# Row maxima of latent attention taken over pairs of key blocks, with ScalarE's positive part between TensorE and VectorE

## The chip, the cores and the metric

The kernel runs on one core of a Trainium2 chip. The metric is the device time of one execution in microseconds (us). A program is timed in several runs, and the median is given. One more execution is recorded by the profiler; its span runs from the first to the last instruction of the core.

The core has TensorE (PE, matrix products into PSUM; "PEld" are its weight loads), VectorE (DVE), ScalarE (ACT), GpSimd (POOL), and SyncE (SP), which issues transfers. Each works through its own queue in order and waits for others by semaphores.

## The reference

Eight blocks of a small hybrid network run on x of shape (2, 1024, 128), each with a layer norm in front and the residual added behind. The first one is a causal latent attention, and the change lies in it alone:

```
q      = einsum('bld,dhk->blhk', x, Wq)              # 16 heads of 64
latent = einsum('bld,dc->blc', x, Wkv_down)          # 32 values per token
k, v   = latent through Wk_up, Wv_up                 # per head
attn   = softmax(where(key <= query, q.k / 8, min))  # over the keys
out    = (attn . v) through Wout
```

It is followed by a spiking feed-forward block, a state-space block, the spiking block again, a linear attention, an expert feed-forward, an attention with 16 heads of 8, and the experts again. All is in float32.

## The kernel before

The keys' up-projection is folded into the queries, so that a head's score is a product over the 32 latent values. Four heads (`J = 4`) lie on the 128 partitions, 32 each, and there are four such groups (`C = 4`). `qT[b]` holds the folded queries of batch b as (4 heads x 32) x group x 1024 tokens. `latT[b]` holds the latent values, repeated for the four heads, as 128 x 1024.

Softmax needs the maximum of each row of scores first. `row_maxima(b, seq, ps, together)` computes them for one batch and is the function that is changed. It goes over the eight query blocks `i` of 128 tokens (`TPB = 8`), the four groups `c`, and the keys up to the diagonal, `nk = (i + 1) * 128`, in halves of at most 512. One round of the innermost loop is called a step here; there are 48 for a batch, and each ends in a `yield`. In a step:

- TensorE makes the scores of four heads (line 265), 128 queries x up to 512 keys each, every head in its own bank of PSUM. The four heads use different rows of the array. In the trace, each of these float32 products is two instructions.
- If the half holds the diagonal block, TensorE adds the causal mask there (line 274): a product of an identity and a matrix that is -3.0e38 above the diagonal, both bf16.
- VectorE takes the negated maximum over the keys out of PSUM (line 283), for `together` heads in one instruction, and writes it into `nm`.

At the end of the batch, the two halves are merged (line 288), the maxima are split into three bf16 terms (lines 294 and 297) and transposed by TensorE into `nmT` (lines 301 and 302). `attend` then computes the scores again, transposed, adds `nmT` to them on TensorE (lines 355 and 364) and takes the exponentials on ScalarE (line 378).

The function is used twice.

- **Batch 0**: `together = 4`, two PSUM tiles of four banks. Nothing else is to be done then, and a scheduler orders the instructions.
- **Batch 1**: `together = 2`, three PSUM tiles of two banks, two of which a step needs. The order is written out by hand (`tc.manual_schedule`): `weave(into_space(0, bank), maxima, 1.1)` takes 1.1 steps of the maxima after each step of the first state-space work. That work has layer norms on VectorE and POOL, the spiking block's products with their activations (`f_ph` line 549, lines 551 and 552 on ScalarE, `f_py` line 557, thresholds on VectorE in line 569), and the state-space projections (`s_pm` line 618, evacuated by ScalarE in lines 678, 689 and 693 and by VectorE in lines 680, 687 and 698; step sizes in lines 705 to 715). Each engine gets its instructions in the order in which the two streams are drawn. What stands behind a waiting instruction in a queue waits too.

Everything behind the two stretches follows after them: `attend` of batch 0 after batch 0's maxima, and the state-space loop with `attend` of batch 1 after batch 1's.

Of the kernel before, what the change touches and what calls it, by code (L numbers as in the profile page):

```python
# [9 lines left out]
F32 = mybir.dt.float32  # L10
BF16 = mybir.dt.bfloat16
AF = mybir.ActivationFunctionType
ALU = mybir.AluOpType
AX = mybir.AxisListType
ENG = mybir.EngineType
PSUM = bass.MemoryType.PSUM
# [3 lines left out]
P = 128  # L20
# [4 lines left out]
TPB = L // P  # L25
# [103 lines left out]
def drain(steps):  # L129
    for _ in steps:  # L130
        pass
# [20 lines left out]
class LatentAttention:  # L152
# [3 lines left out]
    C, J, LD = 4, 4, 32  # L156
# [92 lines left out]
    def row_maxima(self, b, seq, ps, together):  # L249


        nc, C, J = self.g.nc, self.C, self.J
        qT, latT = self.qT[b], self.latT[b]

        nm = seq.tile([P, 2, TPB, C * J], F32, name="a0_nm")
        for i in range(TPB):
            nk = (i + 1) * P
            for c in range(C):
                for half, n0 in enumerate(range(0, nk, 512)):
                    n = min(nk - n0, 512)  # L260
                    last = n0 + n == nk
                    ss = [ps.tile([P, together, 512], F32, name="a0_s", tag="a0_s") for _ in range(J // together)]
                    for j in range(J):
                        quad = slice(32 * j, 32 * j + 32)
                        nc.tensor.matmul(  # L265
                            ss[j // together][:, j % together, :n],
                            qT[quad, c, bass.ts(i, P)],
                            latT[quad, n0 : n0 + n],
                            start=True,
                            stop=not last,  # L270
                        )
                    if last:
                        for j in range(J):
                            nc.tensor.matmul(  # L274
                                ss[j // together][:, j % together, n - P : n],
                                self.identb,
                                self.mask,
                                start=False,
                                stop=True,
                            )  # L280
                    for k, s in enumerate(ss):
                        h = c * J + k * together
                        nc.vector.tensor_reduce(  # L283
                            nm[:, half, i, h : h + together], s[:, :, :n], AX.X, ALU.max, negate=True
                        )
                    yield
        two = TPB // 2
        nc.vector.tensor_tensor(nm[:, 0, two:, :], nm[:, 0, two:, :], nm[:, 1, two:, :], ALU.min)
        terms = seq.tile([P, TPB, P], BF16, name="a0_terms")
        nc.gpsimd.memset(terms, 0.0)  # L290
        rest = nm[:, 0].rearrange("p i (c j) -> p i j c", c=C)
        for t in range(3):
            part = terms.rearrange("p i (j r) -> p i j r", j=J)[:, :, :, t : 3 * C : 3]
            nc.vector.tensor_copy(part, rest)
            if t < 2:
                left = seq.tile([P, TPB, J, C], F32, name=f"a0_left{t}")
                nc.vector.tensor_sub(left, rest, part)
                rest = left
        pt = ps.tile([P, TPB, P], BF16, name="a0_mt", tag="a0_s")
        for i in range(TPB):  # L300
            nc.tensor.transpose(pt[:, i, :], terms[:, i, :], self.identb)
        nc.vector.tensor_copy(self.nmT[b], pt.rearrange("p a b -> p (a b)"))
        yield
# [1183 lines left out]
def first_layer(g, w, open_experts, load_expert):  # L1487

    tc = g.tc

    def pool(stack, name, bufs, **kw):
        return stack.enter_context(tc.tile_pool(name=name, bufs=bufs, **kw))
# [7 lines left out]
    latent = LatentAttention(g, w, pool(latents, "a0_keep", 1, **right))  # L1500
    own = pool(latents, "a0_batch1", 1, **right)
    with ExitStack() as es:
        latent.project([pool(es, "a0_batch0", 1), own])
        with tc.tile_pool(name="a0_seq", bufs=1) as seq, tc.tile_pool(name="a0_ps_a", bufs=2, space=PSUM) as ps:
            drain(latent.row_maxima(0, seq, ps, 4))
        work = pool(es, "a0_work", 2)
        ps, ps_o = pool(es, "a0_ps_b", 3, space=PSUM), pool(es, "a0_ps_o", 1, space=PSUM)
        with tc.manual_schedule(engines=ALL):
            drain(latent.attend(0, work, ps, ps_o, added=True))
# [3 lines left out]
    seq = pool(spaces, "s_seq", 2)  # L1513
    dram = pool(spaces, "s_dram", 2, space=bass.MemoryType.DRAM)
    space = [StateSpace(g, w, b, shared, seq, dram) for b in range(B)]
# [40 lines left out]
    with tc.manual_schedule(engines=ALL):  # L1556
# [8 lines left out]
        ps, ps_o = pool(latents, "a0_ps_b", 2, space=PSUM, **right), pool(latents, "a0_ps_o", 1, space=PSUM, **right)  # L1565
# [23 lines left out]
def kernel(ctx: ExitStack, tc: tile.TileContext, d: dict, out: bass.AP):  # L1589
# [34 lines left out]
    def load_expert(e):  # L1624
        for name in ("Wg", "Wu"):
            nc.sync.dma_start(out=w[name][:, e, :], in_=d[name][e])
        nc.sync.dma_start(out=w["Wd"][:, e], in_=d["Wd"][e].rearrange("(c p) o -> p c o", p=P))

    first_layer(g, w, open_experts, load_expert)
    layer0.close()  # L1630
    heads_and_experts(g, w, [4, 5, 6, 7], [0, 1, 2, 3, 4, 5])
# [69 lines left out]
```

## Time and profile before

| | |
|---|---|
| median of 3 runs | 2143.78 us (2140.81 to 2145.67) |
| profiled execution: time, span | 2140.26 us, 2138.3 us |
| granted TensorE clock, mean | 0.941 of full speed |
| busy in the span: PE, DVE, ACT, POOL | 1849.9, 1590.4, 1145.6, 920.0 us |
| batch 0's maxima: first reduce to last reduce's end | 50.8 to 138.8 us |
| batch 1's maxima, woven into state-space work | 283.8 to 439.4 us |
| reduces of line 283, both batches | 144, 168.2 us busy on DVE |
| score products of line 265 | 768 matmul instructions, 118.1 us busy on PE |

Busy time is the time in which an engine has an instruction under way; register, branch and semaphore instructions do not count. The chain of waits follows the work that ended last back through the time and names at each place the engine that was waited for. A row of a group gives line, engine, operation, output and input with their shapes, the count, the busy time, the mean length of one in ns, and the engine's idle time before them with what ended it. In a stretch's row, the columns are busy time of PE, PEld, DVE, ACT and POOL, the granted clock, the share of the DMA engines and GB/s. Names in the profile leave out numbers: `a_s` are the score tiles, `a_nm` the maxima.

### The profile page before, as it was taken

The page shows a single profiled execution, that of the slowest core. Times are in us where ns is not written, and L with a number is a line of the kernel's source. Part 1 is how long each engine was busy: PE and PEld are TensorE (multiplying, and loading weights), DVE is VectorE, ACT ScalarE, POOL GpSimd, SP SyncE. Part 2 cuts the span into 40 slices and gives each one's busy share as a digit, 9 for nine tenths or more (in the row PEclk, how much of TensorE's full clock was granted, in tenths as well). Part 3 has the DMA queues.
Part 4 walks back from the last instruction along what each step waited for, and adds up shares of the span by engine and source line. Part 5 has one row for each costly group of instructions (what it writes and reads, how often), then busy time and mean ns, then how long its engine had stood idle before and what let it go on. Part 6 is the DMA issues. An engine that isn't in the chain of part 4 may idle for free.

```text
span 2138.3 us, 33736 instructions
## 1 busy us (share of the span) xinstructions
PE 1849.9 (87%) x13632; PEld 1063.0 (50%) x13632; DVE 1590.4 (74%) x1842; ACT 1145.6 (54%) x1577; POOL 920.0 (43%) x510
## 2 busy tenths in 40 slices
PE   7679978979977757899678899999899999998899
PEld 4223243323334422334356566676666666666753
DVE  5876866799765679896432798999899899998222
ACT  1016612266632457773433677777777777777422
POOL 1013411045321210000110288989889889998300
PEclk9979978989987978999899999999999999999999
DMA  4000000087653077660000466666666666666000
GB/s 93 1 1 2 1 1 1 10 208 180 157 117 118 11 166 178 157 151 7 0 1 0 110 177 160 176 178 175 162 173 175 173 175 177 173 178 172 11 5 6
DMA packets 73788, 220.00 MB, mean 103 GB/s; under 512 B 9184, under 2 KB 19872, under 8 KB 73504
## 3 DMA queue, kind: packets, MB, share of 16 engines
q1 hardware_dynamic: 54736, 149.40, 24.0%
q0 software_dynamic: 18432, 67.12, 16.5%
q8 instruction: 107, 1.75, 0.4%
q10 hardware_dynamic: 464, 1.33, 0.3%
q14 instruction: 49, 0.40, 0.1%
HBM read 78.35 MB, written 5.24 MB: 39 GB/s over the span
## 4 chain that ended last, share of the span: by engine, by line
PE 47%; DVE 28%; issue 8%; POOL 7%; ACT 5%; DMA 4%; SPq 0%; DVEq 0%; POOLq 0%; ACTq 0%
DVE h_e L1281 5%; DVE h_m L1275 5%; DVE a_nm L283 4%; POOL h_e L1331 4%; PE h_s L1264 4%; DVE s_h L792 3%; PE a_st L355 3%; PE a_s L265 3%; DMA h_e<-h_e 3%; PE e_pgu L1053 3%; PE e_pg L955 3%; PE e_pu L956 3%; PE e_po L971 3%; PE h_po L1111 3%; PE s_pm L618 3%
## 5 line engine op out<-in xcount | busy, mean ns | idle before, releaser
L1331 POOL TENSOR_TENSOR h_e<-h_e,h_r 128x2048 f32<-128x2048 f32 x128 | 601.5, 4705 | 76.3 <-ACT h_r L1324 42.4
L1284 ACT ACTIVATE h_e<-h_e 128x1024 f32<-128x1024 f32 x256 | 256.6, 1049 | 165.7 <-DVE h_e L1281 165.0
L1275 DVE TENSOR_REDUCE h_m<-h_s 128x128 f32<-128x2048 f32 x128 | 293.2, 2291 | 53.5 <-PE h_s L1264 50.7
L1281 DVE TENSOR_TENSOR h_e<-h_s,h_m 128x2048 f32<-128x2048 f32 x128 | 293.2, 2290 | 8.7
L381 POOL TENSOR_SCALAR_AFFINE_SELECT a_pT<-a_pT 128x256 f32<-128x256 f32 x120 | 126.0, 1071 | 209.2 <-ACT a_pT L378 206.3
L283 DVE TENSOR_REDUCE a_nm<-a_s 128x2 f32<-128x1024 f32 (+7 forms) x144 | 168.2, 1217 | 43.0 <-PE a_s L274 26.5
L1264 PE MATMUL h_s<-h_qz,h_kT 32*128 32x512 f32 x1024 | 148.0, 646 | 43.5 <-DVE h_e L1281 43.3
L1111 PE MATMUL h_po<-e_h,Wd 128*128 128x256 f32 x640 | 172.8, 389 | 4.0 <-DVE e_h L1070 1.6
L378 ACT ACTIVATE a_pT<-a_st 128x1024 f32<-128x1024 f32 (+3 forms) x176 | 129.9, 791 | 64.2 <-PE a_st L364 63.0
L792 DVE TENSOR_TENSOR_SCAN s_h<-s_a,s_h 128x1024 f32<-128x1024 f32 x64 | 148.9, 2326 | 18.4 <-ACT s_a L760 14.4
L1292 POOL DMA_DIRECT2D h_e<-h_e x128 | 132.1, 1032 | 60.5 <-DMA h_e<-h_e 43.6
L1297 PE MATMUL h_pd<-ident,h_e 128*128 128x128 f32 x1024 | 138.9, 279 | 19.9 <-DMA h_e<-h_e 13.9
L1297 PEld LDWEIGHTS h_pd<-ident,h_e 128*128 128x128 f32 x1024 | 114.2, 142 | 80.8 <-DMA h_e<-h_e 34.9
L265 PE MATMUL a_s<-a_latT,a_qT 32*128 32x512 f32 (+3 forms) x768 | 118.1, 600 | 39.8 <-DVE a_nm L283 37.8
L1336 PE MATMUL h_po<-h_e,h_vz 128*32 128x128 f32 x4096 | 139.8, 277 | 0.7 <-POOL h_e L1331 0.6
L355 PE MATMUL a_st<-a_qT,a_latT 32*128 32x512 f32 (+3 forms) x768 | 121.0, 562 | 11.2 <-ACT a_pT L378 9.0
L1111 PEld LDWEIGHTS h_po<-e_h,Wd 128*128 128x128 f32 x640 | 112.4, 193 | 31.2 <-DVE e_h L1070 16.0
L958 ACT ACTIVATE e_sg<-e_pg 128x512 f32<-128x512 f32 x96 | 57.3, 597 | 129.5 <-PE e_pg L955 107.3
L963 DVE TENSOR_TENSOR e_h<-e_sg,e_pu 128x512 f32<-128x512 f32 x96 | 64.5, 683 | 82.3 <-PE e_pu L956 70.2
L1336 PEld LDWEIGHTS h_po<-h_e,h_vz 128*32 128x32 f32 x4096 | 104.9, 110 | 33.3 <-issue 31.6
L956 PE MATMUL e_pu<-e_uT,Wu 128*128 128x512 f32 x192 | 102.1, 614 | 19.0 <-DVE e_h L963 19.0
L1084 PE MATMUL e_pgu<-e_uT,Wg 128*128 128x256 f32 x480 | 116.0, 382 | 0.0
(298 smaller groups left out, 3264.1 us busy)
## 6 DMA issues: line engine op xcount, KB each, us to landing
h_e<-h_e SPq DMA_DIRECT2D x128, 512.0 KB, 3.9
h_e<-h_e POOLq DMA_DIRECT2D x128, 512.0 KB, 5.0
s_a<-s_steps SPq DMA_DIRECT2D x64, 512.0 KB, 4.9
s_h<-s_steps SPq DMA_DIRECT2D x64, 512.0 KB, 6.5
s_steps<-s_gate SPq DMA_DIRECT2D x8, 256.0 KB, 2.0
Wg<-in_Wg_dram SPq DMA_DIRECT2D x8, 256.0 KB, 6.0
Wu<-in_Wu_dram SPq DMA_DIRECT2D x8, 256.0 KB, 5.9
Wd<-in_Wd_dram SPq DMA_DIRECT2D x8, 256.0 KB, 6.1
```

The costliest lines, as they stand in the source:

```text
L265: nc.tensor.matmul(ss[j // together][:, j % together, :n], qT[quad, c, bass.ts(i, P)], latT[quad, n0 : n0 + n], start=True, stop=not last,)
L283: nc.vector.tensor_reduce(nm[:, half, i, h : h + together], s[:, :, :n], AX.X, ALU.max, negate=True)
L355: nc.tensor.matmul(ss[j // 2][:, j % 2, off:], latT[quad, bass.ts(kb, P)], qT[quad, c, q0 : q0 + n], start=True, stop=False,)
L792: nc.vector.tensor_tensor_scan(h, a, h, 0.0, ALU.mult, ALU.add)
L1111: nc.tensor.matmul(self.sums, self.w["Wd"][:, e, fc, :], h, start=False, stop=last, skip_group_check=True)
L1264: nc.tensor.matmul(s[:, j, :].rearrange("p (k q) -> p k q", k=K), kTs[b][quad, bass.ts(kb, P)], qzs[b][qb // 4][quad, :, bass.ts(qb % 4, P ...
L1275: nc.vector.tensor_reduce(m, heads.rearrange("p h q -> p q h"), AX.X, ALU.max)
L1281: nc.vector.tensor_sub(e, heads, m.unsqueeze(1).to_broadcast([P, H, P]))
L1284: nc.scalar.activation(eh, eh, AF.Exp, scale=scale)
L1297: nc.tensor.matmul(pd[:, t, :], pair[:, t, k, :], g.ident, start=(t == 0 and k == 0), stop=(k == 7), is_transpose=True, skip_group_check=True,
L1331: nc.gpsimd.tensor_mul(e, e, r.unsqueeze(1).to_broadcast([P, H, P]))
L1336: nc.tensor.matmul(po[32 * j : 32 * j + 32, :], vz[:, kb * J + j, k].rearrange("p a d -> p (a d)"), a[:, 4 * j + k, :], start=False, stop= ...
```

## The change

The maximum of two scores a and b is a + max(b - a, 0). The keys are taken in pairs of blocks of 128. For each pair TensorE makes the scores of the first block and, in a second product, the differences of second and first: the keys of that product are differences of the latent values, `rises`, which POOL computes once for a batch. ScalarE takes the positive part of the differences out of PSUM into `up`, and one VectorE instruction for each head adds it to the first block's scores, negates, and takes the minimum over the pair's 128 columns into `nm`. A head's tile holds the first blocks' scores in columns 0 to 255 of its bank and the differences in columns 256 to 511, so a step has at most two pairs. The causal mask is added to the difference of the last pair, whose second block is always the diagonal one. For an odd query block, the pairs are (0,1), (2,3) and so on. For an even one, they are block 0 by itself with a difference of zero, then (1,2), (3,4) and so on; `firsts` holds the first blocks of that case. Query block 0, with one key block, keeps products, mask and reduce. The number of steps of a batch stays at 48.

For batch 0, `together` becomes 2 and the PSUM tiles become four of two banks. Batch 1's call keeps three tiles of two banks.

```diff
-        for i in range(TPB):
-            nk = (i + 1) * P
+        blocks = latT.rearrange("p (m two k) -> p m two k", two=2, k=P)
+        even, odd = blocks[:, :, 0, :], blocks[:, :, 1, :]
+        firsts = seq.tile([P, 4, P], F32, name="a0_firsts")
+        rises = [seq.tile([P, 4, P], F32, name=f"a0_rises{n}") for n in range(2)]
+        nc.gpsimd.tensor_sub(rises[1], odd, even)
+        nc.gpsimd.memset(rises[0][:, 0, :], 0.0)
+        nc.gpsimd.tensor_sub(rises[0][:, 1:, :], even[:, 1:, :], odd[:, 0:3, :])
+        nc.scalar.copy(firsts[:, 0, :], even[:, 0, :])
+        nc.scalar.copy(firsts[:, 1:, :], odd[:, 0:3, :])
...
+        for i in range(1, TPB):
+            pairs = i // 2 + 1
+            first, rise = even if i % 2 else firsts, rises[i % 2]
             for c in range(C):
-                for half, n0 in enumerate(range(0, nk, 512)):
+                for half, m0 in enumerate(range(0, pairs, 2)):
+                    m = min(pairs - m0, 2)
+                    last = m0 + m == pairs
...
+                    for part, keys in enumerate((first, rise)):
+                        for j in range(J):
+                            quad = slice(32 * j, 32 * j + 32)
+                            nc.tensor.matmul(
+                                ss[j // together][:, j % together, 256 * part : 256 * part + m * P],
+                                qT[quad, c, bass.ts(i, P)],
+                                keys[quad, m0 : m0 + m, :],
+                                start=True,
+                                stop=not (part and last),
+                            )
                     if last:
...
                     for k, s in enumerate(ss):
-                        h = c * J + k * together
-                        nc.vector.tensor_reduce(
-                            nm[:, half, i, h : h + together], s[:, :, :n], AX.X, ALU.max, negate=True
-                        )
+                        up = seq.tile([P, together, 256], F32, name="a0_up", bufs=4)
+                        nc.scalar.activation(up[:, :, : m * P], s[:, :, 256 : 256 + m * P], AF.Relu)
+                        for j in range(together):
+                            h = c * J + k * together + j
+                            nc.vector.tensor_tensor_reduce(
+                                out=up[:, j, : m * P],
+                                in0=s[:, j, : m * P],
+                                in1=up[:, j, : m * P],
+                                scale=-1.0,
+                                scalar=3.0e38,
+                                op0=ALU.add,
+                                op1=ALU.min,
+                                accum_out=nm[:, half, i, h : h + 1],
+                            )
                     yield
...
-        with tc.tile_pool(name="a0_seq", bufs=1) as seq, tc.tile_pool(name="a0_ps_a", bufs=2, space=PSUM) as ps:
-            drain(latent.row_maxima(0, seq, ps, 4))
+        with tc.tile_pool(name="a0_seq", bufs=1) as seq, tc.tile_pool(name="a0_ps_a", bufs=4, space=PSUM) as ps:
+            drain(latent.row_maxima(0, seq, ps, 2))
```

The lines left out of the loop are the tile allocation and the mask product (now at column `256 + (m - 1) * 128`), and query block 0's own copy of products, mask and reduce.

## The prediction

> **What bounds the kernel now.** I read the chain of waits first, for the two stretches in which row maxima are computed: batch 0's alone, and batch 1's woven into the first state-space work.
>
> ```profile
> by line: DVE a_nm L283 76.0%; PE a_s L265 20.3%; PE a_s L274 2.5%; issue 1.0%; DVE a_nm L288 0.3%; DVEq L283 0.0%
> ```
> ```profile
> by line: PE a_s L265 30.7%; PE s_pm L618 22.4%; DVE a_nm L283 13.1%; PE a_s L274 5.9%; PE f_ph L549 5.1%; PE f_py L557 4.5%; DVE f_cnt L569 3.4%; PE a_st L459 1.9%; PE s_pt L137 1.6%; PE a_st L446 1.3%; issue 1.1%; DVE ln_st L62 0.9%; PE f_
> ```
> ```profile
> 50.00:139.00 89.00, 59.23 (x512) 24.50 (x512) 81.71 (x49) 0.00 (x0) 0.22 (x1) 0.89 0.00 1
> ...
> 282.00:330.00 48.00, 40.50 (x224) 19.92 (x224) 32.39 (x73) 6.78 (x10) 9.16 (x12) 0.75 0.00 1
> 330.00:380.00 50.00, 42.33 (x226) 19.33 (x226) 34.93 (x52) 11.32 (x16) 7.39 (x9) 0.86 0.00 0
> 380.00:440.00 60.00, 55.78 (x234) 19.64 (x232) 50.09 (x56) 13.51 (x17) 0.00 (x0) 0.95 0.11 33
> ```
>
> The first line is the chain over 50 to 139 us: VectorE's reduces are it. The second covers 276 to 442 us: there TensorE's queue is the chain, and the reduces only 13%. The third view gives busy time by stretch (PE, weight loads, DVE, ACT, POOL, then the granted clock): in batch 0 VectorE is full and ScalarE idle; in batch 1 PE and VectorE both come near the stretch's length, and the clock falls to 0.75.
>
> Next, by shape, the rows that price the change (mean ns after the busy time):
>
> ```profile
> L283 DVE TENSOR_REDUCE a_nm<-a_s 128x2 f32<-128x1024 f32 x48 | 56.4, 1218 | 17.7 <-PE a_s L265 10.7 <-PE a_s L274 7.0
> L283 DVE TENSOR_REDUCE a_nm<-a_s 128x4 f32<-128x2048 f32 x24 | 54.0, 2285 | 5.6 <-PE a_s L265 5.2
> ...
> L1070 DVE TENSOR_TENSOR e_h<-e_sg,e_pgu 128x256 f32<-128x256 f32 x80 | 33.7, 421 | 94.2 <-ACT e_sg L1061 94.2
> ...
> L1445 DVE TENSOR_TENSOR x_res<-x_res,h_po 128x128 f32<-128x128 f32 x16 | 4.5, 278 | 6.6 <-ACT h_po L1117 6.6
> ...
> L74 DVE TENSOR_SCALAR l_nb<-l_mv,l_rs 128x1 f32<-128x1 f32 x32 | 4.2, 205 | 8.5 <-POOL l_rs L68 8.5
> ...
> L713 DVE SCALAR_TENSOR_TENSOR s_delta<-s_z,s_ln 128x512 f32<-128x512 f32 x4 | 2.7, 682 | 0.0
> ...
> L41 DVE MEMSET power<- 128x1 f32 x1 | 0.1, 59 | 0.9 <-PEq L1691 0.9
> ```
>
> Last, the timeline: how an instruction with an accumulator follows another (start, length), and how closely short reduces follow each other.
>
> ```profile
> 755.05 0.69 ACT L863 ACTIVATE l_kT<-l_pm,l_nmax 128x512 f32<-128x512 f32 x1 [0.52 <-DVE l_nmax L860]
> 755.64 0.19 ACT L863 ACTIVATION_READ_ACCUMULATOR l_kT<-l_pm,l_nmax 128x1 f32 x1
> 755.73 0.68 ACT L863 ACTIVATE l_kT<-l_pm,l_nmax 128x512 f32<-128x512 f32 x1
> ...
> 356.96 0.76 DVE L283 TENSOR_REDUCE a_nm<-a_s 128x2 f32<-128x256 f32 x2 [2.07 <-PE a_s L274]
> ```
>
> Two reduces of 415 ns end within 0.76 us, so the second starts 0.345 us after the first: VectorE overlaps 70 ns. On ScalarE the accumulator read starts 0.10 us before its ACTIVATE ends, and holds the queue for 0.09 us.
>
> **The instructions.** Per batch and head, the reduces read 128 x 36 = 4608 columns. Afterwards query block 0 keeps its reduce (128 columns; 8 of two heads), and query blocks 1 to 7 take pairs: 11 halves x 4 groups = 44 steps, 32 of two pairs (256 columns) and 12 of one (128). A step has two Relu activations and four fused instructions: 176 per batch, 128 of 256 columns and 48 of 128. In the instruction order each of them is followed by a second VectorE instruction of one column, which writes `nm`. So VectorE reads 2560 columns per head, but runs 8 + 352 instructions where 48 or 96 stood.
>
> **The pair's price** (fused instruction and its read) is not in the trace. The nearest rows are L1070 and L1445, one input from PSUM and one from SBUF. Taken: 421 - 70 + 95 = 446 ns for 256 columns and 278 - 70 + 95 = 303 for 128, the read costing about what ScalarE's read does. Cheapest, with the memset's 59 for the read: 410 and 267. Dearest, nothing overlapped and L74's 205: 626 and 483. I take the middle since back-to-back instructions overlap in every such row.
>
> The Trainium skill (Vector Engine (DVE) Microarchitecture Reference, Points that are easy to get wrong) says that this instruction family with two non-bf16 SBUF sources runs at half rate; if that held here it would add 0.267 us x 128 + 0.133 x 48 = 40 us per batch. The change's first input is in PSUM, and L713, of that family with both inputs in SBUF, took 682 ns for 512 columns, full rate. The same page (Measured stream behaviour on trn2) gives about 75 ns per instruction besides 1.04 per column, for such programmed instructions too; by it a pair would be 418 and 284 ns, and batch 0's VectorE work 69.8 us where the next paragraph has 74.4.
>
> **Batch 0.** VectorE: 128 x 0.446 + 48 x 0.303 + 8 x 0.345 = 57.1 + 14.5 + 2.8 = 74.4 us (cheapest 68.1, dearest 106.6) for 82.8 now (54.0 + 13.7 + 9.6 + 5.5). From first reduce (50.8) to last end (138.8) it is 88.0 us, 5.2 of it idle. Others stay under: Relu 64 x 0.591 (L551) + 24 x 0.381 (L378) = 47 us; TensorE, by the timeline's 0.43 us for eight 256-column matmuls, 0.31 for eight weight loads and 0.33 for four masks, 47 us at full clock, 53 at 0.89.
>
> The new wait is the Relu between scores and maximum. Two steps are in flight (four tiles). From the release of a step's second tile: 0.21 + 0.21 us of matmuls, 0.28 tail, up to 0.37 for the mask, 0.1 of hand-overs, 0.60 of Relu: 1.4 to 1.8 us against 1.78 for the other step's four pairs. It just fits. Steps of one pair are about 0.2 us late, 12 x 0.2 = 2.4, so I put 3 us idle: 77.4, a change of **-10.6 us** (-16 to +20). The three new Pool operations (about 3 us; L467's 512-column add took 1.58) and ScalarE's two copies lie beside block 0's steps; without that cover they would cost those 3 us once.
>
> **Batch 1.** The queues are written out by hand, and three tiles serve steps of two, so a step's second half waits for the release of the step before. Queued behind that matmul on PE is the state-space product; behind VectorE's wait for Relu stands state-space arithmetic; behind ScalarE's wait for scores stand the spiking and size activations. From release to release, for 512 key columns: now 0.43 + 0.28 + 1.22 us, 0.33 more with a mask, but two reduces take 2.35, which sets it. Afterwards 0.43 + 0.28 + 0.60 + 0.15 + 0.89 = 2.35, or 2.72 with the mask, with only 1.78 of it VectorE's. By block:
> - Block 7 (416.1 to 439.4, 8 steps of 2.9 us, VectorE full): 2.65 each, -2.
> - Block 6 (8 steps of 2.5 us): 2.65, +1.2.
> - Blocks 4 and 5 are slower for other reasons (3.5 us per step). Beside f_ph's two activations (L551 and L552, 1.22 us) two Relus make ScalarE's share 2.4 us where a step took 2.1: 8 x 0.3 = +2.4.
> - TensorE: block 2 has 512 columns per head for 384, 4 x 0.21 / 0.71 = +1.2. One-pair steps wait for weights, 0.62 us for 0.31 to 0.43: 12 x 0.25 = 3, two thirds of it on the chain, +2.
>
> Together **+5 us**. Above: all 32 wide steps pay the loop's 0.37, with the rest +18. Below: VectorE's relief (87.2 to 74.4 us, in its 22 us of this chain) -3, with block 7 -5.
>
> **Sum.** -10.6 + 5 = -5.6 us on the profiled execution's 2140.3 (span 2138.3): 2134.7. The median of the runs, 2143.8, lies 3.5 above that execution, so 2138. Downstream nothing is moved: each stretch ends in one transpose on which the next begins.
>
> **Rivals.**
> 1. *The pair runs in series (slower).* Each nanosecond per pair costs 176 ns in batch 0 and, with two pairs on the loop in 44 steps, 88 in batch 1: 0.264 us. The gain is gone at 21 ns over 446; over 483 ns the kernel is slower by more than 0.2%. If the read waits for the fused instruction's end (421 + 95 = 516), +18.5, +13 in sum: 2157; at the dearest price 2185. For it: two dependent instructions 352 times, none seen here. Against: L863's overlap. 0.30.
> 2. *The hand-written queues decide.* Batch 1 pays its upper bound, 18: +7, 2151. For it: the chain there is TensorE's, and it gets more columns, more weight loads and a longer loop. Against: PE and VectorE both idle in that stretch now. 0.12.
> 3. *Cheaper pairs (410) and a hidden loop.* -16, and block 7's -2 without the other additions: 2126. 0.18.
>
> My forecast has the remaining 0.40. That the change does not do what it says is excluded by the order of instructions: the column count does fall by 44%.
>
> **Chances.** 0.2% (4.3 us) is about what a measurement can tell from no change. The forecast's own range is 2132 to 2145: of its 0.40, 0.26 is faster by more, 0.12 within, 0.02 slower. Rival 3 gives 0.18 faster, rivals 1 and 2 give 0.04 within and 0.38 slower: 0.44, 0.16, 0.40. The range runs from rival 3, 2124, to 2172, between rival 1's two prices; the ends that both unknowns at their worst would make, 2120 and 2197, are left out.
>
> **What would show it.** In batch 0 the first TensorReduce to the last fused instruction lasts 77 us, ScalarE is busy 47, and VectorE's idle time there is about 3 us, put down to ScalarE. A fused instruction of 256 columns reads about 420 ns, and the next one starts 446 after. Batch 1's stretch is 5 us longer, with waits of `a_s` matmuls for `a_nm` grown. I am wrong if pairs are over 480 ns apart, or if batch 1's stretch moves by more than 10 us.

## The result, and the profile after

The changed kernel takes 2148.5 us (median of 20 runs, 2142.4 to 2152.9); the kernel before, run beside it, 2140.6 (20 runs). The ratio is 1.0038, with a 95% interval of 1.0028 to 1.0048: slower, by 7.9 us in the medians. The forecast was 2138, faster. The profiled execution took 2148.8 us (span 2146.8).

First the groups of the changed lines by shape (count, then busy time and mean ns, then idle time before them). The change moves later lines by 41; line 314 is the positive part, 317 the fused instruction and its read, 296 the score products, 305 the mask.

```profile
L317 DVE CUSTOM_DVE_ANT_0 a_up<-a_s,a_up 128x256 f32<-128x256 f32 x256 | 92.7, 421 | 68.5 <-ACT a_up L314 68.2
L314 ACT ACTIVATE a_up<-a_s 128x512 f32<-128x512 f32 x128 | 69.5, 594 | 79.8 <-issue 53.4 <-PE a_s L296 16.2 <-PE a_s L305 5.1
L317 DVE DVE_READ_ACCUMULATOR2_ANT a_nm<- 128x1 f32 x352 | 29.2, 83 | 0.0
```

The timeline of VectorE inside batch 0 (start, length):

```profile
111.51 0.42 DVE L317 CUSTOM_DVE_ANT_0 a_up<-a_s,a_up 128x256 f32<-128x256 f32 x1 [0.83 <-ACT a_up L314]
111.86 0.08 DVE L317 DVE_READ_ACCUMULATOR2_ANT a_nm<- 128x1 f32 x1
111.86 0.42 DVE L317 CUSTOM_DVE_ANT_0 a_up<-a_s,a_up 128x256 f32<-128x256 f32 x1
```

A fused instruction reads 421 ns, but the next one starts 0.345 us after it, at the same moment as the read of the accumulator, which costs nothing: in the prediction's timeline two reduces of as many columns follow each other after 0.345 us too, without such a read. The 0.83 us in brackets is what is new: VectorE idle, until ScalarE has the positive part.

Busy time by stretch (PE, weight loads, DVE, ACT, POOL, then the clock), batch 0 first, then three parts of batch 1's woven stretch; and who waited for whom, longest sums first, in batch 0 (first two lines) and in the woven stretch (the others):

```profile
49.00:128.00 79.00, 70.38 (x864) 53.89 (x864) 60.10 (x361) 43.19 (x90) 2.67 (x4) 1.00 0.01 2
267.00:315.00 48.00, 37.38 (x292) 23.27 (x292) 27.87 (x124) 13.33 (x27) 11.52 (x15) 0.75 0.00 1
315.00:365.00 50.00, 42.96 (x332) 24.20 (x330) 25.90 (x132) 23.56 (x45) 5.22 (x7) 0.90 0.01 1
365.00:440.00 75.00, 64.29 (x410) 33.86 (x410) 40.45 (x190) 36.19 (x60) 2.15 (x2) 0.82 0.08 24
```
```profile
DVE a_up L317 <- ACT a_up L314: 17.3, 25, 0.9
PEld a_s L296 <- ACT a_up L314: 10.8, 18, 0.8
```
```profile
DVE a_up L317 <- ACT a_up L314: 70.3, 39, 4.4
...
PEld a_s L296 <- ACT a_up L314: 25.9, 26, 1.9
...
PE a_s L296 <- DVE a_nm L317: 18.0, 16, 4.2
```

In batch 0 VectorE fell from 82 us busy to 60, TensorE rose to 70, and no engine is full. In batch 1 VectorE is busy for half of the time, and both it and TensorE wait for ScalarE.

Cut at the first merge of maxima, the first residual of `attend`, the second merge, and the first and last work of the heads-and-experts phase, two executions of each kernel give (us; the second ones are from the experiments below):

| | before | before, again | after | after, again |
|---|---|---|---|---|
| batch 0: first reduce to merge | 88.0 | 87.6 | 78.0 | 80.1 |
| attend of batch 0 | 142.8 | 139.4 | 139.1 | 142.1 |
| batch 1, woven, to its merge | 157.9 | 157.4 | 172.8 | 169.0 |
| to the heads phase | 744.5 | 744.4 | 745.8 | 742.3 |
| heads and experts | 823.1 | 825.4 | 828.7 | 825.6 |

Batch 0 gained 7 to 10 us, batch 1 gave back 12 to 15. What follows has the same instructions in the same order in both kernels; its differences are as large between two executions of one kernel.

**TensorE's clock.** In the trace's records the granted clock is 1.0 or 0.5, never between, and changes after multiples of 3.41 us. A state-space product of 512 columns is recorded with 0.59 us at full clock and with 1.06 at half. So I split a stretch's time into TensorE's idle time, its busy time at full clock, and a loss: half of the busy time that fell in half-clock stretches. This split is used below, from batch 0's merge to batch 1's (attend and woven stretch together, "merge to merge").

### The profile page after: what moved, and what is told of

It is laid out like the page before. It is cut to its first block, busy times and chain, and to the rows that moved or that the text cites. A ratio compares the mean times of both kernels' runs of the same rounds, so it can differ in the third digit from the quotient of the medians.

```text
span 2146.8 us, 36231 instructions
## 1 busy us (share of the span) xinstructions
PE 1868.5 (87%) x14336; PEld 1116.8 (52%) x14336; DVE 1546.0 (72%) x2418; ACT 1230.9 (57%) x1757; POOL 924.8 (43%) x516
## 3 DMA queue, kind: packets, MB, share of 16 engines
q1 hardware_dynamic: 54736, 149.40, 23.7%
## 4 chain that ended last, share of the span: by engine, by line
PE 38%; DVE 22%; issue 8%; POOL 6%; ACT 6%; DMA 5%; SPq 0%; DVEq 0%; POOLq 0%; ACTq 0%
DVE h_m L1316 5%; DVE h_e L1322 5%; DMA h_e<-h_e 4%; PE h_s L1305 4%; POOL h_e L1372 4%; DVE s_h L833 3%; PE e_pgu L1094 3%; PE e_pg L996 3%; PE e_pu L997 3%; PE e_po L1012 3%; PE h_po L1152 3%; PE s_pm L659 2%; PE e_pgu L1125 2%; PE a_st L396 2%; DVE s_h L832 2%
## 5 line engine op out<-in xcount | busy, mean ns | idle before, releaser
L317 DVE CUSTOM_DVE_ANT_0 a_up<-a_s,a_up 128x256 f32<-128x256 f32 (+1 forms) x352 | 114.3, 384 | 87.8 <-ACT a_up L314 87.6
L314 ACT ACTIVATE a_up<-a_s 128x512 f32<-128x512 f32 (+1 forms) x176 | 85.3, 536 | 104.2 <-issue 63.0
```

## The experiments

Theory 1: in batch 1 the positive part, by its place between TensorE and VectorE, lengthens the time until a score tile is free. Theory 2: a quicker batch 0 is paid back by a lower clock behind it. Theory 3: TensorE's added columns, products and weight loads do it.

**One batch at a time.** Both versions of `row_maxima` are kept, and one call takes the old one:

```diff
-            maxima = latent.row_maxima(1, aseq, ps, 2)
+            maxima = latent.row_maxima_reduce(1, aseq, ps, 2)
```

> Batch 0 takes its maxima over pairs as in the changed kernel (two heads per tile, four tiles); batch 1 keeps the reduces of the kernel before. Theory 1 (in batch 1's woven stretch the positive part stands in ScalarE's queue between scores and maximum, and the release of the three tiles takes longer): batch 0's maxima last 78 us for 88, attend of batch 0 a few us less, the woven stretch stays at 158 us, in all -10 to -15 us: ratio 0.993 to 0.995, about 2127 us. Theory 2 (the quicker batch 0 is paid back by a lower granted clock in the stretch behind it): the woven stretch lasts 163 to 173 us with the old reduces too, at a clock of about 0.82 for 0.86; ratio 0.998 to 1.004. The phase of heads and experts, unchanged, shows by how much it moves with its start alone: 823 to 829 us.

> Batch 0 keeps the reduces (four heads per tile, two tiles); batch 1 takes its maxima over pairs as in the changed kernel. Theory 1: the woven stretch lasts about 173 us for 158, +15 us: ratio 1.006 to 1.008, about 2155 us. Theory 2: with batch 0 as slow as before the clock is 0.86 again and the stretch 160 to 166 us: ratio 1.001 to 1.004.

Batch 0 alone: 2134.4 us, ratio 0.9964 (0.9952 to 0.9976). That is less than theory 1 expected, since the maxima took 80.1 us and `attend` stayed at 141.8. The woven stretch with the old reduces lasts 156.5 us at the old clock, 0.86. Batch 1 alone: 2152.1, 1.0052 (1.0032 to 1.0072); woven stretch 169.3. Theory 2 falls: the stretch is long by its own pairs, whatever batch 0 did.

**Without the positive part in batch 1.**

```diff
-    nc.scalar.activation(up[:, :, : m * P], s[:, :, 256 : 256 + m * P], AF.Relu)
+    if b == 0:
+        nc.scalar.activation(up[:, :, : m * P], s[:, :, 256 : 256 + m * P], AF.Relu)
...
-    in1=up[:, j, : m * P],
+    in1=(up if b == 0 else level)[:, j, : m * P],
```

(`level` is a tile of zeros.)

> The changed kernel, but in batch 1 no positive part is taken: the fused instruction adds a tile of zeros that is set once, so that part of batch 1's maxima is left out. TensorE's additional columns, matmuls and weight loads, and VectorE's 352 instructions, remain. Theory 1: without ScalarE between scores and maximum the woven stretch goes back to 158 us or below (150 to 158): ratio to the kernel before 0.990 to 0.995. Rival (TensorE's added work makes the stretch longer, or the clock does): it stays at 168 to 173 us, ratio about 1.002.

2120.9 us, 0.9910 (0.9893 to 0.9928). The woven stretch, with all of the new products and fused instructions, lasts 145 us, 28 less than in the changed kernel:

```profile
269.00:414.00 145.00, 127.03 (x1036) 72.95 (x1034) 92.79 (x441) 31.33 (x42) 19.48 (x25) 0.89 0.03 10
```

Theory 3 falls too: the same products fit in there (1036 matmul instructions on record, 1032 in the changed kernel). PE's busy time is 18 us less, 14 of them because it runs at half clock for a shorter time (the mean clock is 0.89 instead of 0.82).

**ScalarE's work, or its place?** Three attempts to divide theory 1, and a smaller tile:

```diff
-    in1=up[:, j, : m * P],                              # unread: ScalarE's line stays as it is
+    in1=(up if b == 0 else level)[:, j, : m * P],
```
```diff
-    for part, keys in enumerate((first, rise)):
+    for part, keys in ((1, rise), (0, first)):          # differences, mask, first blocks
```
```diff
-    nc.scalar.activation(self.gate[:, e, cols], pm, AF.Silu)
+    nc.scalar.activation(self.gate[:, e, cols], pm, AF.Relu)   # likewise for Exp and Ln
```
```diff
-    maxima = latent.row_maxima(1, aseq, ps, 2)          # three tiles of two heads
+    maxima = latent.row_maxima(1, aseq, ps, 1)          # six tiles of one head; batch 0: eight
```

> The changed kernel with the positive part of batch 1 still computed on ScalarE, but read by nobody: batch 1's fused instructions add zeros, so that part of its maxima is left out. VectorE no longer waits for ScalarE; a tile is still released only when both have read it. Measured from batch 0's merge of maxima to batch 1's merge (attend included): 311.9 us in the changed kernel, 284.2 without the positive part, 300.6 in the kernel before. Theory 1a (the serial hand-over scores, positive part, fused instruction lengthens the loop over three tiles): the two readers now overlap, 0.6 to 0.9 us less in each of 44 steps, 284 to 293 us. Theory 1b (the positive part comes late because it stands behind state-space work in ScalarE's queue, and the tile waits for it): little changes, 302 to 310 us.

> The changed kernel with the products of a step in the other order, in both batches: differences and mask first, then the first blocks' scores. Same work on all engines; the positive part can start while TensorE makes the scores. Theory 1a: 0.2 to 0.4 us less in each of batch 1's 44 steps, 9 to 17 us: merge to merge 295 to 303 us for 311.9; batch 0's maxima 72 to 76 us for 78. In all ratio to the kernel before 0.993 to 0.998. Theory 1b: merge to merge stays at 307 to 313 us, ratio 1.001 to 1.004.

> The changed kernel, with the state-space block's Silu, Exp and Ln in front of its loop replaced by functions that load no table (Relu, Abs, Identity), so that its values are not the reference's; the seven table loads of 1.28 us in the woven stretch go. Theory 1b: the positive parts and the activations behind them come earlier, merge to merge 9 to 14 us shorter than 311.9, 298 to 303 us. Theory 1a: table loads are 7 of some 130 ScalarE instructions there, and merge to merge falls by 0 to 5 us.

> The changed kernel with one head per PSUM tile in both batches: eight tiles in batch 0, six in batch 1, one positive part per head. Theory 1a: batch 1's tiles come free one head earlier, which shortens the loop by one fused instruction and half a positive part, 0.35 + 0.25 us in 44 steps, against some 0.1 us more ScalarE work for each step: merge to merge 290 to 302 us for 311.9. Theory 1b: ScalarE has 88 more instructions, merge to merge 308 to 316 us. Batch 0 as with batch 0 alone and eight tiles: 77 us.

Unread: merge to merge 308.9 us, ratio 1.0032 (1.0016 to 1.0049). The run does not decide between theories 1a and 1b: VectorE still waited 68 us for ScalarE. The program puts the two readers of a PSUM tile in order, one behind the other, whether or not the second needs the first's result.

Differences first: 2165.0 us, 1.0115 (1.0091 to 1.0139), where either theory had expected at most 1.004; batch 0's maxima took 85.8 us, merge to merge 322.5. The timeline, in batch 0, shows why it did not help:

```profile
117.60 0.28 PE L305 MATMUL a_s<-a_mask,a_identb 128*128 128x128 bf16 x2
117.81 0.71 PE L296 MATMUL a_s<-a_firsts,a_qT 32*128 32x256 f32 x8
118.61 2.07 ACT L314 ACTIVATE a_up<-a_s 128x512 f32<-128x512 f32 x4 [1.98 <-issue]
```

Differences and mask are done at 117.9, but ScalarE starts at 118.61, when the first blocks' scores have ended too: TensorE announces a tile once, after its last product. And a masked step's product instructions now run as four differences, two masks, four differences, two masks, eight firsts: a cycle of two steps takes 4.05 us for 3.68 (from one start of ScalarE's four to the next).

No table loads (with other functions in their place): 310.8 us merge to merge, 1.0030 (1.0016 to 1.0045). The seven loads are not the cost.

One head per tile: 2130.0 us, 0.9949 (0.9931 to 0.9967). Merge to merge 303.4, between the two ranges and 8.5 less than the changed kernel: TensorE's idle time is back at 30.9 us, its clock is not better. That speaks for the hold of the tile.

**The two things that ScalarE's place means: the tile is held, and the queues wait.** First neither, then one and the other, as far as they come apart. In the first run ScalarE works on a constant tile in both batches. In the second the fused instructions go first and ScalarE reads the tile behind them. In the third VectorE does what ScalarE did there.

```diff
+    nc.scalar.activation(up[:, :, : m * P], level[:, :, : m * P], AF.Relu)         # first: from SBUF
...
+    nc.scalar.activation(up[:, :, : m * P], s[:, :, 256 : 256 + m * P], AF.Relu)   # second: behind the loop over j
...
+    nc.vector.tensor_scalar(up[:, :, : m * P], s[:, :, 256 : 256 + m * P], 0.0, None, ALU.max)   # third
```

> The changed kernel with ScalarE taking the positive part of a constant tile in SBUF, as often and as wide as before, in both batches, and the fused instructions adding zeros: the positive part of the differences is left out of the maxima. ScalarE has the same work in the same places of its queue, but waits for no scores, holds no PSUM tile, and VectorE does not wait for it. From batch 0's merge to batch 1's merge (300.6 us in the kernel before, 311.9 in the changed one, 308.9 with the positive part computed but unread, 284.2 without it). Theory 1c (the tile is held until ScalarE has read it, TensorE waits for its release, and its clock falls to half more often): 284 to 290 us, TensorE idle 30 us for 40. Theory 1d (ScalarE's added 42 us of work delays the state-space activations behind it): 300 to 309 us. Batch 0's maxima: 62 to 68 us if VectorE's wait for ScalarE sets them, 75 to 79 if TensorE's products do.

> The changed kernel, but in batch 1 VectorE's fused instructions come first and add zeros (the positive part is left out of batch 1's maxima), and ScalarE takes the positive part of the differences out of the same tile after them, read by nobody. VectorE waits for the scores alone; the tile is held for as long as in the changed kernel, in the other order. Merge to merge (311.9 us in the changed kernel, 308.3 with batch 1 alone, 284.2 without the positive part): if the hold of the tile is the cost, 303 to 312 us; if it is VectorE's queue that waits for ScalarE (70 us of such waits in the changed kernel) and holds up the state-space arithmetic behind it, 284 to 295 us.

> As the run with the positive part after the fused instructions, but VectorE itself takes it (maximum with zero, 512 columns, about 0.6 us per tile, read by nobody; the positive part is left out of batch 1's maxima). The tile is held for some 0.75 + 0.6 us, as in the changed kernel, and ScalarE is not in it at all; VectorE has some 53 us more work, 145 of it in the stretch. Merge to merge: if the hold of the tile is the cost, 300 to 312 us; if ScalarE's and VectorE's queues waiting for each other are, 286 to 297 us.

The woven stretch of the three kernels, in this order:

```profile
260.00:404.00 144.00, 126.79 (x1032) 72.61 (x1032) 92.28 (x441) 71.44 (x130) 19.45 (x25) 0.91 0.03 11
```
```profile
267.00:431.00 164.00, 138.10 (x1035) 76.30 (x1033) 93.24 (x441) 74.23 (x128) 19.47 (x25) 0.86 0.03 10
```
```profile
269.00:444.00 175.00, 144.64 (x1036) 81.14 (x1035) 137.84 (x530) 31.37 (x42) 19.48 (x25) 0.81 0.04 12
```

| merge to merge, us | in all | TensorE idle | half-clock loss | busy at full clock |
|---|---|---|---|---|
| before; again | 300.6; 296.9 | 31.2; 31.2 | 29.4; 25.4 | 240.0; 240.4 |
| after; again | 311.9; 311.1 | 40.1; 40.8 | 31.9; 30.2 | 239.9; 240.1 |
| no positive part | 284.2 | 30.2 | 17.7 | 236.3 |
| positive part of a constant | 286.3 | 29.9 | 20.3 | 236.1 |
| positive part behind the fused ones | 303.2 | 38.3 | 23.7 | 241.2 |
| the same on VectorE | 313.9 | 42.4 | 30.1 | 241.4 |
| one head per tile, both batches | 303.4 | 30.9 | 33.1 | 239.4 |

ScalarE's 40 us of added work cost some 2 us (286.3 for 284.2), no more than two executions of one kernel can differ by (2113.4 us in all, ratio 0.9872, 0.9852 to 0.9891). ScalarE's read of the tile behind the fused instructions costs 19 us (284.2 to 303.2), though VectorE never waits for the positive part there; that VectorE does wait adds the other 8. In that run, however, ScalarE waited 68 us for VectorE, so both the tile and ScalarE's queue are held up. With VectorE as the second reader and ScalarE out of it, the stretch is as long as in the changed kernel; but VectorE has 45 us more work there, and what stands behind it in VectorE's queue waits too. So the place costs, and not ScalarE's work; how much of the 27 us is the hold of the tile, and how much the queues behind it, is not shown. The two runs took 2140.3 us (1.0000, 0.9983 to 1.0016) and 2150.5 (1.0048, 1.0031 to 1.0065). Of the 27 to 28 us between no positive part and the changed kernel, 10 are idle time of TensorE, 12 to 14 its clock, and 4 more busy time. Against the kernel before, the changed one is 11 to 14 us longer from merge to merge: 9 to 10 of them are idle time of TensorE, 2 to 5 its clock, and the busy time at full clock is the same.

**Batch 0's floor, and better versions.** Batch 0 with one head per tile; the same with batch 1 by reduces of one head per tile; batch 0 by pairs without the positive part:

```diff
-        with tc.tile_pool(name="a0_seq", bufs=1) as seq, tc.tile_pool(name="a0_ps_a", bufs=4, space=PSUM) as ps:
-            drain(latent.row_maxima(0, seq, ps, 2))
+        with tc.tile_pool(name="a0_seq", bufs=1) as seq, tc.tile_pool(name="a0_ps_a", bufs=8, space=PSUM) as ps:
+            drain(latent.row_maxima(0, seq, ps, 1))
```

> As batch 0 alone, but with eight PSUM tiles of one head each instead of four of two heads, and one positive part for each head (twice as many ScalarE instructions, half as wide). VectorE was idle for about 18 us of batch 0's 78 us, mostly waiting for ScalarE. If that comes from the coarse hand-over (a tile's two heads wait for one another), batch 0's maxima last 64 to 72 us and the kernel is 6 to 12 us below the version with batch 0 alone; if it comes from ScalarE's or TensorE's throughput, they last 76 to 85 us.

> Batch 0 by pairs with one head per PSUM tile (eight tiles), batch 1 by the reduces of the kernel before, but with one head per PSUM tile too (six tiles, 192 reduces more narrow by half for 96). Theory 1c: a tile is held for one reduce of 0.61 us instead of one of 1.22, TensorE idles less and its clock falls less: merge to merge 285 to 295 us for 298 to 301 with two heads per tile; in all ratio to the kernel before 0.990 to 0.994, 2120 to 2128 us. Rival (VectorE's 96 more instructions and TensorE's own work set the stretch): 297 to 303 us, ratio 0.995 to 0.997.

> Batch 0 by pairs with four tiles of two heads, but its fused instructions add zeros and ScalarE does nothing, so that the positive part is left out of batch 0's maxima; batch 1 by the reduces of the kernel before. If VectorE's wait for the positive part makes the 18 us of idle time in batch 0's 78 us, they last 60 to 66 us here; if TensorE's 352 + 352 products and their weight loads do, they last 73 to 79 us. Batch 1 from merge to merge as with batch 0 alone: 298 us.

Single heads in batch 0: 76.7 us for the maxima, in the range expected if throughput sets them; 2131.3 us in all, 0.9956 (0.9940 to 0.9973). With single reduces in batch 1: 2130.6, 0.9945 (0.9925 to 0.9965); merge to merge 297.9, so the finer release gains nothing there, as the rival said. Batch 0 without the positive part (2125.3 us in all, 0.9926, 0.9911 to 0.9941): 67.1 us, 1 us above the first range, with TensorE full:

```profile
50.00:118.00 68.00, 66.08 (x864) 50.28 (x856) 60.09 (x362) 0.19 (x1) 2.82 (x4) 0.95 0.01 2
```

So of batch 0's 78 to 80 us, 67 are left with TensorE full (3 of them half-clock loss), and ScalarE's place makes 11 to 13. ScalarE's work is not the cost here either: with the positive part of a constant, batch 0 lasted 67.1 us too. Four versions leave nothing out and beat both kernels: batch 0 alone by pairs, the same with single heads, with single reduces in batch 1, and pairs with single heads in both batches. They take 2130.0 to 2134.4 us, which their intervals do not tell apart.

**Repeats.**

> The kernel before, once more, for its phases: the phase of heads and experts lasted 823.1 us in its profiled execution and 825 to 833 us in those of seven kernels that have the same code there, with TensorE's work at full clock 746 to 747 us in all of them. If those 5 us are the chance of where the half-clock windows fall, another execution of the kernel before gives some value between 823 and 833; if the change or the size of the program makes them, it gives 822 to 824 again. Ratio 1.000.

> The changed kernel once more. The phases of a second execution: batch 0's maxima 78 to 80 us, batch 1's woven stretch 169 to 173 (by where TensorE's half-clock windows fall), heads and experts 823 to 833. Ratio 1.003 to 1.005 as before; 1.000 to 1.003 if the parts add up to the whole.

> Batch 1 by pairs, batch 0 by reduces, once more. If parts add up, the ratio is that of the changed kernel plus batch 0's 0.0036: 1.006 to 1.008; its first six runs gave 1.0052 (1.0032 to 1.0072).

Before: ratio 0.9990 (0.9973 to 1.0007), heads phase 825.4. After: 1.0028 (1.0012 to 1.0044), heads phase 825.6. So the 5.6 us that the first two executions differed by there lie within the spread between executions. Batch 1 alone: 1.0054 (1.0033 to 1.0074). The parts give 0.9964 x 1.0053 = 1.0017, the whole 1.0028 and 1.0038: the intervals overlap, and whether some 3 us of interplay remain stays open.

## Why the prediction was wrong

**Batch 1's term failed.** It said +5 us, with +18 as a bound; the woven stretch grew by 14.9 and, in the second executions, 11.6, beyond the 10 us that the prediction gave as its own sign of being wrong. The mechanism was named (tiles released later, behind one more engine), but the step was mis-sized. The new loop was compared with the old limit, which it exceeded by 0.37 us where a mask comes and by nothing elsewhere. Blocks 6 and 7 then got 2.65 us for a step, without a working, and in block 7 that was set down as a gain. By query block, from the last maximum of one to that of the next, after against before:

| block | predicted | measured, 1st and 2nd executions |
|---|---|---|
| 7 | -2 | +4.8, +1.4 |
| 6 | +1.2 | +4.0, +4.0 |
| 1, 4 and 5 | +2.4, and +2 for one-pair steps | +3.9, +3.7 |
| 2 | +1.2 | +2.1, +2.1 |
| 0 and 3 | 0 | +0.1, +0.5 |

The last row hides two changes: block 3 is 1.9 and 1.6 us shorter, block 0 some 2 us longer.

Block 6 has no half-clock time in the kernels compared here, so it shows the loop by itself: 23.0 us before, 27.0 after, 21.7 without the positive part and 21.7 with that of a constant. So a step took 2.88 us before, not the 2.5 of the prediction, and takes 3.38 now; my 2.65 is about what it takes without the positive part (2.71). The positive part's place costs (27.0 - 21.7) / 8 = 0.66 us in every step. That is near one positive part's 0.59 and a hand-over, but TensorE's records divide it otherwise: of the 5.3 us, 2.0 are its idle time (2.6 for 0.6), and 2.9 are its score products, which are the same and are under way for 12.2 us instead of 9.3. The scores of one step without the positive part (first two lines), and of one in the changed kernel:

```profile
385.97 0.71 PE L299 MATMUL a_s<-a_firsts,a_qT 32*128 32x256 f32 x8
386.51 0.61 PE L299 MATMUL a_s<-a_rises,a_qT 32*128 32x256 f32 x8
...
396.19 1.03 PE L296 MATMUL a_s<-a_firsts,a_qT 32*128 32x256 f32 x6
396.75 0.48 PE L296 MATMUL a_s<-a_rises,a_qT 32*128 32x256 f32 x2
397.02 0.41 PE L296 MATMUL a_s<-a_firsts,a_qT 32*128 32x256 f32 x2
397.06 0.80 PE L296 MATMUL a_s<-a_rises,a_qT 32*128 32x256 f32 x6
```

The first two lines last 1.15 us, the other four 1.67: the four heads' products no longer run together. Without the positive part five of the block's steps take the 1.15 us, in the changed kernel two, and the others there up to 1.81. I read this as the step's second tile coming free later than its first; no run tests that by itself. What the sum also left out, though the prediction names it, is that the next scores start only when TensorE's in-order queue comes to them, behind a state-space product (`s_pm`, 1.1 to 1.9 us in the timeline there). I took the longest of several limits for the step where parts of them add up; that reading is argued, too. VectorE's relief in block 7 was there to be had (20.1 us without the positive part, for 23.9 before), but in the changed kernel VectorE waited for ScalarE.

**The clock was not in the sum.** Windows of 3.4 us in block 7 of the changed kernel, and ScalarE's and TensorE's timeline around the first of them:

```profile
408.20:411.60 3.40, 2.02 (x21) 1.32 (x20) 2.07 (x9) 2.15 (x5) 0.00 (x0) 1.00 0.00 0
411.60:415.10 3.50, 2.56 (x18) 1.67 (x17) 3.17 (x11) 2.56 (x4) 0.00 (x0) 0.51 0.00 0
415.10:418.50 3.40, 3.40 (x7) 1.14 (x4) 1.49 (x9) 1.08 (x2) 0.00 (x0) 0.50 0.01 2
418.50:421.90 3.40, 1.90 (x25) 1.31 (x28) 1.10 (x7) 1.67 (x3) 0.00 (x0) 1.00 0.01 2
421.90:425.30 3.40, 3.40 (x20) 1.88 (x19) 0.94 (x7) 1.08 (x2) 0.00 (x0) 0.50 0.00 0
```
```profile
406.38 0.63 ACT L746 ACTIVATE s_v<-s_z 128x512 f32<-128x512 f32 x1 [1.71 <-DVE s_z L739]
407.02 1.28 ACT L747 ACT_TABLE_LOAD   x1
408.32 0.63 ACT L747 ACTIVATE s_v<-s_v 128x512 f32<-128x512 f32 x1
408.86 1.06 ACT L314 ACTIVATE a_up<-a_s 128x512 f32<-128x512 f32 x2
...
410.39 0.48 PE L296 MATMUL a_s<-a_latT,a_qT 32*128 32x256 f32 x2 [1.38 <-DVE a_nm L317]
```

A positive part stands behind a state-space activation, a table load and a second activation and starts at 408.86; TensorE, waiting for the tile, is busy for 2.02 of 3.40 us, and in the next window its clock is half. The window from 418.5 repeats it. So the waits can cost more than their own length. The Trainium skill (TensorE: Matmul & The Clock Gate, Part 1) describes such a clock: one that is full or half, by activity in free-running windows of 3413 ns; the records here agree (1.0 or 0.5, changes after multiples of 3.41 us). Its section on HAM oscillation puts the rule as no idle gaps above some 3.4 us. Here the longest gap in the window from 408.2 was 1.4 us, and the clock fell all the same. But the busy share of a window does not decide it either. In batch 0 of the kernel before, TensorE was busy for 1.60 to 1.75 us in each of five windows in a row (75.6 to 92.6 us), all at full clock, and the clock fell only behind the fifth. One of them:

```profile
79.00:82.40 3.40, 1.69 (x20) 0.94 (x20) 2.73 (x3) 0.00 (x0) 0.00 (x0) 1.00 0.00 0
```

What makes the clock fall is not shown by these runs. Where the windows fall differs between executions: block 7 had 17.1 us at half clock in one of the changed kernel and 6.8 in the other, and the heads phase, with the same work in each kernel (746 to 748 us busy at full clock), lasted 823 to 833 us.

**Batch 0's term came out by luck: two errors cancel.** -10.6 us was predicted (77.4); measured 78.0 and 80.1, for 88.0 and 87.6. The pair was too dear: 446 ns for 256 columns, with 410 as the cheapest bound, where 345 were measured, below both. VectorE is busy for 60.1 us instead of 74.4. The idle time was too small: 3 us instead of some 18. The sum of hand-overs had TensorE at 47 us and taken as hidden; it needs 67 with nothing else in the way. Had I had the pair's price right and kept the rest, the forecast would have been further off.

**The rivals.** Rival 1, the pair in series, is wrong in its price: the read of the accumulator does not even take its turn. Rival 3 has the cheap pair right and the hidden loop wrong. Rival 2, that the queues decide and batch 1 pays its bound of 18, gave 2151 us; the measured 2148.5 is that rival with batch 1 paying 12 to 15 and batch 0 gaining 7 to 10. It stood at 0.12 with the argument that PE and VectorE both idle in that stretch; in the changed kernel both wait for ScalarE there (the lines above), which speaks for it. The sign of faster and slower was what the 0.40 on the forecast's own path got wrong; the time lay within the range. The prediction's sums have small slips that change none of this: the bounds -16 and +20 of batch 0 work out to -17 and +22, the bound +18 of batch 1 to 17.4, and rival 3 is 2126 us in one place and 2124 in another. "Downstream nothing is moved" holds within the spread between executions.

## What to carry to other kernels

Before putting a free engine between two that are handing over buffers, count for how long each buffer is held and what stands in the producer's queue between two uses: in a loop over few buffers an added stage can cost about its own length in every round (0.66 us a step in block 6, for a positive part of 0.59), even if no engine is full. An idle engine in a profile is no reserve as long as the wait that ends its idle time is a buffer's release. And a change that helps where an engine is the limit (batch 0) should be tried there alone: the same code in the woven stretch, where VectorE was not the limit, turned 8 us of gain into 8 of loss. A smaller tile can make up for it: with one head per tile, pairs in both batches were as good as pairs in batch 0 alone.

## What the runs showed of the hardware that was not expected

- The read of VectorE's accumulator costs no time: its row of 83 ns starts with the next fused instruction, and pairs of 256 columns follow each other every 345 ns, as two reduces of 256 columns without a read do. The Trainium skill (Vector Engine (DVE) Microarchitecture Reference, Measured stream behaviour on trn2) gives 1.04 ns per column and about 75 ns per instruction: an estimate of 341 ns for the fused instruction, which agrees, and 75 more for the read, which is not seen.
- TensorE's clock fell to half after windows of 3.4 us in which it was busy for about 0.6 of the time (2.02 and 1.90 of 3.40 us), and stayed there for two windows and more; elsewhere four windows with about 0.5 left it at full clock. In the woven stretch the half-clock loss was 13 us without the positive part, 27 and 22 in the two executions of the changed kernel, and 20 in both of the kernel before.
- The same score products of block 6, at full clock in both kernels, were under way for 12.2 us instead of 9.3 once the positive part stood behind them.
